# A cross-attention kernel: keys and values by seven quarter products instead of full products, with the work around them spread anew

## The chip, the cores and the metric

The kernel runs on one core of a Trainium2 chip. The metric is the device time of one execution in microseconds (us). Before the change it was 1430.49 us, the median of three runs (1426.22 to 1430.94).

A core has engines that run side by side, each with an instruction queue of its own: TensorE (PE, matrix products; PEld is its weight load), VectorE (DVE), ScalarE (ACT), GpSimd (POOL), and SyncE (SP), whose queue issues the loads and stores here. Data lies in on-chip memory (SBUF, 128 partitions); products land in banks of PSUM and have to be copied or added out of it by VectorE or ScalarE.

## The reference

Two layers run one after the other over x (8 batches x 512 tokens x 512 features) with a context of 8 x 120 rows of 512 features. Each has a gated cross attention and a gated feed-forward part. Cut to what matters (the layer norms, the residuals and the gates belong to the layers' frame):

```python
def _xattn_ref(query_input, key_input, value_input, key_mask, Wq, bq, Wk, bk, Wv, bv, Wo, bo):
    q = _split_heads(query_input @ Wq.T + bq)      # 16 heads of 32
    k = _split_heads(key_input @ Wk.T + bk)
    v = _split_heads(value_input @ Wv.T + bv)
    scores = jnp.einsum('bhqd,bhkd->bhqk', q, k) / jnp.sqrt(jnp.float32(HD))
    scores = jnp.where(mask == 0, jnp.float32(-1e+30), scores)
    attn = jax.nn.softmax(scores, axis=-1)
    ctx = jnp.einsum('bhqk,bhkd->bhqd', attn, v)
    return ctx.transpose(0, 2, 1, 3).reshape(B, -1, D) @ Wo.T + bo

x = x + tanh(g_xattn) * _xattn_ref(layernorm(x), ctx, ctx, ...)
x = x + tanh(g_ffn) * _ffn(layernorm(x))
```

The first layer's attention has no biases and no mask and its feed-forward part routes tokens to experts; the second layer's attention has both, and its feed-forward part mixes each token with the one before it and forms a gated product of 512 x 512 matrices.

## The kernel before

x stays in SBUF for the whole run, as 32 tiles of 128 tokens. The kernel is a sequence of stages: the first attention, the routed experts, the second attention, the channel mix. Each attention (`CrossAttention`) has three parts: a prologue, a loop over token tiles (`run`, lines 635 to 662) and a tail. The change is about the prologue.

**Order of the work.** The whole constructor of `CrossAttention`, with `load`, `project_keys` and `prologue` in it, stands in a block `tc.manual_schedule(engines=every)` (lines 1402 and 1417): on TensorE, VectorE, ScalarE, GpSimd and SyncE the instructions are issued in the order in which the text writes them. In the loop only TensorE (in the second attention SyncE as well) follows the text; a planner orders the other engines by its own costs.

**Loads (`load`, line 263).** The context comes in two halves of four batches (480 rows), then weights and biases. In the first attention the context has to be turned (features onto the partitions) by TensorE (`turn_context`, line 362), and the turned context is written aside to HBM (line 360). The second attention (`self.turned`) loads it from there, twice: into `ctx` for the keys, in two halves, and into `ctxT` for the values. Tiles of the prologue lie in two pools, `at_v` and `at_k`, that begin at the upper end of the memory and reuse the room of the experts' tiles, `permT` (16 KB a partition), `hT` and weights; a load waits until the last reader of what lay there is done.

**Keys (`project_keys`, line 333).** For each half and each of four groups of 128 features: four matmuls of 128 x 128 weights by 480 context rows, summed in one PSUM bank (`kps`, L345), and a copy by ScalarE with the factor 1/sqrt(32) (L354, L358). TensorE runs each of these float32 matmuls as two instructions, so a half has 32.

**Values (`project_values`, line 375).** For each batch four matmuls, 120 context rows by 512 weight columns (`vps`, L379), and an eviction by VectorE, with the bias added in the second attention (L388, L390). After it come the statistics (`bn_stats`, `bn_aggr`, L49 and L50) of four token tiles, and GpSimd's four small instructions for their scales (L58 to L64). In `prologue` three batches come first, three stand between the token tiles' transposes, and the last two come after the scores of token tile 0, between its two parts.

**Queries by seven products.** `SevenProducts` (line 72) multiplies two 512 x 512 matrices, cut into quarters, by seven products of quarters instead of eight, with sums of quarters in front (S1 to S4, `left_steps`; T1 to T4, `right_steps`, each four instructions) and sums behind. Each product, p1 to p7, is four matmuls (eight instructions) into one bank. They run in the order 1, 2, 6, 5, 7, 4, 3. p1 (A11, B11) and p2 (A12, B21) need no sums; p6 needs S2 and T2, the third of the four instructions on each side. p1 and p5 are copied out by ScalarE; p2, p6, p7, p4 and p3 are added by VectorE; after p7 GpSimd adds p5 to two quarters (L192, L193); p4's subtraction has to wait for the first of these and p3's addition for the second. The queries (`queries`, line 465) use it from the start: the weights' sums are made by GpSimd (`sum_query_weights`, L88), the tokens' sums (`start_queries`, L107) by VectorE for the first two batches.

**Tokens.** `normalize` (line 420) has ScalarE write the normalized tile; with biases GpSimd then adds the gated output bias to x (L428). `transpose_x` (line 431) has TensorE turn the tile and ScalarE copy it out (L440). When a batch's four tiles are turned, its query sums follow.

**Scores.** `scores` (line 483) computes the scores of one token tile into the two double banks `s`, VectorE takes the maxima (L532, L543) and subtracts (L545), ScalarE exponentiates (L535, L546). The banks are free for the next scores, or for the transposes of the probabilities (`tps`, L564), only when L535 and L545 have read them. `p_mm` has four further banks, which everything else takes in turn.

## Time and profile before

The profiled execution took 1431.72 us; its span, from the first to the last instruction, is 1429.9 us, and the mean granted TensorE clock 0.995 of full speed.

| what | measured |
|---|---|
| median of three runs | 1430.49 us |
| first attention: first turn of the context to the scores of tile 1 | 9.19 to 91.37 us |
| second attention: first key matmul to the scores of tile 1 | 693.25 to 768.91 us |
| key matmuls of one attention (`kps`, L345, second attention) | 64 in 26.03 us |
| value matmuls of one batch (`vps`, L379) | 8 in 3.43 us |
| TensorE busy from 104 to 200 us, in the first loop | 95.0 of 96.0 us |
| TensorE busy from 790 to 900 us, in the second loop | 110.0 of 110.0 us |

How to read the lines that follow in this document. A page gives the busy time of each engine and its share of the span; the chain that ended last is followed back from the last instruction, at each step to what released it. A line of the instructions in order of time has the start (us from the span's start), the length, the engine, the line of the kernel, the operation, output tile <- input tiles, the shape, and in brackets the idle time of the engine before it with what ended it. Matmuls are pipelined, so the times of single ones overlap; the distance from start to start is what counts.

### The profile page before, as it was taken

The page shows a single profiled execution, that of the slowest core. Times are in us where ns is not written, and L with a number is a line of the kernel's source. Part 1 is how long each engine was busy: PE and PEld are TensorE (multiplying, and loading weights), DVE is VectorE, ACT ScalarE, POOL GpSimd, SP SyncE. Part 2 cuts the span into 40 slices and gives each one's busy share as a digit, 9 for nine tenths or more (in the row PEclk, how much of TensorE's full clock was granted, in tenths as well). Part 3 has the DMA queues.
Part 4 walks back from the last instruction along what each step waited for, and adds up shares of the span by engine and source line. Part 5 has one row for each costly group of instructions (what it writes and reads, how often), then busy time and mean ns, then how long its engine had stood idle before and what let it go on. Part 6 is the DMA issues. An engine that isn't in the chain of part 4 may idle for free.

```text
span 1429.9 us, 32488 instructions
## 1 busy us (share of the span) xinstructions
PE 1383.4 (97%) x13696; PEld 1067.2 (75%) x13696; DVE 1020.5 (71%) x1453; ACT 768.2 (54%) x1870; POOL 644.0 (45%) x576
## 2 busy tenths in 40 slices
PE   7999999999999997999999999999998999999997
PEld 3577777777776787888657777777776788888886
DVE  2666777777777676777566777777777588887786
ACT  1256666666666445444225665666566555445543
POOL 1425545545444000555375575565546333343331
PEclk9999999999999999999999999999999999999999
DMA  9400000000001337432501000000000000000001
GB/s 301 162 9 24 24 23 23 24 23 16 24 31 43 131 125 227 133 106 87 173 0 60 2 2 1 2 2 2 2 30 2 1 30 30 30 30 30 30 16 45
DMA packets 45240, 73.39 MB, mean 51 GB/s; under 512 B 2925, under 2 KB 21869, under 8 KB 44837
## 3 DMA queue, kind: packets, MB, share of 16 engines
q1 hardware_dynamic: 44805, 71.30, 15.0%
q8 instruction: 108, 1.77, 0.5%
q14 instruction: 39, 0.32, 0.1%
q10 hardware_dynamic: 288, 0.00, 0.0%
HBM read 52.55 MB, written 18.74 MB: 50 GB/s over the span
## 4 chain that ended last, share of the span: by engine, by line
PE 72%; DVE 14%; ACT 6%; POOL 4%; issue 3%; DMA 1%; POOLq 0%; SPq 0%; DVEq 0%; ACTq 0%
PE ops L616 15%; PE qps L149 13%; PE tps L564 6%; PE cps L149 5%; PE aps L599 5%; PE s L507 4%; PE kps L345 4%; PE rps L1010 3%; PE vps L379 3%; PE l1ps L925 2%; PE rlps L749 2%; PE ops L1031 2%; PE gps L898 2%; PE xnps L439 2%; DVE rT L990 2%
## 5 line engine op out<-in xcount | busy, mean ns | idle before, releaser
L525 POOL TENSOR_TENSOR pr<-pr,rs 128x960 f32<-128x960 f32 x128 | 229.4, 1795 | 253.2 <-DVE rs L524 231.7
L616 PE MATMUL ops<-wo,aT 128*128 128x512 f32 x512 | 240.6, 596 | 0.7 <-ACT aT L607 0.7
L535 ACT ACTIVATE pr<-s,nmx 128x120 f32<-128x120 f32 x512 | 176.8, 371 | 114.0 <-DVE nmx L532 110.1
L616 PEld LDWEIGHTS ops<-wo,aT 128*128 128x128 f32 x512 | 92.6, 191 | 72.5 <-issue 67.8
L1023 POOL TENSOR_TENSOR r<-r,b 128x1024 f32<-128x1024 f32 x31 | 73.5, 2377 | 145.2 <-ACT r L1022 145.2
L149 PE MATMUL qps<-xnT,wq 128*128 128x256 f32 x512 | 119.6, 381 | 0.0
L564 PEld LDWEIGHTS tps<-ident,pr 128*120 128x120 f32 x864 | 96.7, 138 | 29.6 <-issue 26.2
L543 DVE TENSOR_REDUCE mx<-s 128x8 f32<-128x960 f32 x64 | 74.0, 1156 | 56.6 <-PE s L507 56.6
L535 ACT ACTIVATION_READ_ACCUMULATOR pr<-s,nmx 128x1 f32 x512 | 111.1, 217 | 0.0
L564 PE MATMUL tps<-ident,pr 128*120 128x128 f32 x864 | 104.9, 273 | 2.5 <-ACT pr L535 1.3
L149 PEld LDWEIGHTS qps<-xnT,wq 128*128 128x128 f32 x512 | 95.7, 189 | 15.2 <-issue 1.0
L551 DVE TENSOR_REDUCE sm<-pr 128x8 f32<-128x960 f32 x64 | 73.5, 1148 | 21.9 <-ACT pr L546 21.8
L49 DVE BATCH_NORM_STATS2 bnst<-x 128x6 f32<-128x512 f32 x128 | 86.8, 678 | 1.3
L440 ACT COPY xnT<-xnps 128x512 f32<-128x512 f32 x64 | 38.1, 595 | 82.0 <-PE xnps L439 82.0
L532 DVE TENSOR_REDUCE nmx<-s 128x8 f32<-128x960 f32 x64 | 73.5, 1148 | 8.3 <-PE s L507 8.3
L599 PE MATMUL aps<-prT,v 120*32 120x128 f32 x2048 | 73.3, 278 | 4.1 <-ACT prT L589 2.2
L545 DVE TENSOR_TENSOR pr<-s,mx 128x960 f32<-128x960 f32 x64 | 73.5, 1149 | 0.9
L1276 POOL TENSOR_TENSOR x<-x,cv 128x512 f32<-128x512 f32 x28 | 41.5, 1480 | 70.7 <-DVE cv L1273 70.7
L574 ACT COPY prT<-tps 120x1024 f32<-120x1024 f32 x54 | 55.0, 1019 | 32.7 <-PE tps L564 32.7
L507 PE MATMUL s<-kT,qT 32*128 32x120 f32 x2048 | 71.9, 278 | 0.0
L507 PEld LDWEIGHTS s<-kT,qT 32*128 32x128 f32 x2048 | 66.5, 188 | 6.5 <-issue 6.3
L599 PEld LDWEIGHTS aps<-prT,v 120*32 120x32 f32 x2048 | 53.8, 110 | 18.3 <-issue 8.6
(191 smaller groups left out, 3088.2 us busy)
## 6 DMA issues: line engine op xcount, KB each, us to landing
w<-in_w_dram SPq DMA_DIRECT2D x32, 512.0 KB, 4.8
x<-in_x_dram SPq DMA_DIRECT2D x8, 1024.0 KB, 15.4
aside<-x SPq DMA_DIRECT2D x32, 256.0 KB, 2.0
x<-aside SPq DMA_DIRECT2D x8, 1024.0 KB, 10.5
out_dram<-x SPq DMA_DIRECT2D x14, 512.0 KB, 2.8
wk<-in_wk_dram SPq DMA_DIRECT2D x3, 1024.0 KB, 8.8
wv<-in_wv_dram SPq DMA_DIRECT2D x3, 1024.0 KB, 5.6
wq<-in_wq_dram SPq DMA_DIRECT2D x2, 1024.0 KB, 15.7
```

Of the source, the lines that this page charges most:

```text
L49: cm.nc.vector.bn_stats(st, cm.x[:, t, :])
L149: self.nc.tensor.matmul(ps[:, m, :], self.a[a][:, k, m * P : (m + 1) * P], self.b[b][:, k, :], start=(k == 0), stop=(k == 1),)
L507: nc.tensor.matmul(s[j // 2][:, j % 2, hc * LK : (hc + 1) * LK], self.qT[b][r : r + 32, hc, toks], self.kT[r : r + 32, hc, keys], start=no ...
L525: nc.gpsimd.tensor_tensor(pr[:, js, :, :], pr[:, js, :, :], rs[:, js, :, :].to_broadcast([P, 2, NC, LK]), ALU.mult,)
L532: nc.vector.tensor_reduce(nmx, sv[1], AX.X, ALU.max, negate=True)
L535: nc.scalar.activation(pr[:, 2 + j, hc, :], sv[1][:, j, hc, :], AF.Exp, bias=nmx[:, j, hc, :], accum_out=sm[:, 2 + j, hc : hc + 1],)
L543: nc.vector.tensor_reduce(mx, sv[0], AX.X, ALU.max)
L545: nc.vector.tensor_tensor(pv, sv[0], mx.to_broadcast([P, 2, NC, LK]), ALU.subtract)
L551: nc.vector.tensor_reduce(sm[:, :2, :], pv, AX.X, ALU.add)
L564: nc.tensor.transpose(ps[:, jj, hc * P : (hc + 1) * P], pr[:, 2 * u + jj, hc, :], self.cm.ident,)
L599: nc.tensor.matmul(aps[32 * j : 32 * j + 32, hc, :], self.v[b // 2][:LK, b % 2, h * HD : (h + 1) * HD], prT[:, j, hc, :], start=True, stop ...
L616: nc.tensor.matmul(ops, self.aT[t][:, c, :], self.wo[:, c, :], start=(c == 0), stop=(c == NC - 1),)
```

## The change

- Keys and values are computed with `SevenProducts` too, one object for each half of the context (480 rows): seven products of 256 x 256 weight quarters by 256 x 240 context quarters for the keys (28 matmuls, 56 instructions, of 240 columns, where there were 32 instructions of 480); for the values the context quarter is the stationary side (120 rows, two batches) and the weight quarter the moving one (256 columns). `turned=LK` exchanges the sides.
- New sums: four of the key weights on VectorE, four of each context half on GpSimd (used by keys and values), four of the value weights on GpSimd. New sums behind: GpSimd adds twice after each p7, as for the queries, for two key and two value halves.
- The context is one tile for each half, used by keys and values. The second attention loads it once instead of twice; its second half is loaded behind the biases of queries and keys and the value weights. The write aside in the first attention becomes two.
- The factor 1/sqrt(32) moves from the keys' copy to the tokens' copy (L440) and to the query bias. The value bias of the second attention is added in two parts (one on p1, one after p7, with `bvmore`, the difference of the bias halves); keys and queries use `bias(n)`.
- The statistics no longer come in batches of four tiles: `pieces` puts one or two behind each product. The gated output bias, the normalization of the first two tiles and the query weights' sums move behind the keys or behind the first half of the values.
- All values are computed before the queries. Behind the scores of tile 0, before their softmax, come the transposes and normalizations of three token tiles (`tokens`).
- The query tile is allocated when the batch is turned, and holds T3 until p7; the tile `xns` falls away. The tiles of the attention's second half (`prT`, `aT`) and the channel mix's `r` lie in a pool `late`, opened after the prologue.

```diff
         ps = self.psum()
+        rows, columns, n = self.a[a], self.b[b], P
+        if self.turned:
+            rows, columns, n = columns, rows, self.turned
         for m in range(2):
             for k in range(2):
                 self.nc.tensor.matmul(
                     ps[:, m, :],
-                    self.a[a][:, k, m * P : (m + 1) * P],
-                    self.b[b][:, k, :],
+                    rows[:, k, m * n : (m + 1) * n],
+                    columns[:, k, :],
...
-        for m in range(2):
-            self.nc.scalar.activation(
-                self.q1[:, m, :], ps[:, m, :], AF.Identity, bias=self.bias[0][:, m : m + 1]
-            )
+        else:
+            self.bias[0](self.q1, ps)
     def p2(self):
         ps = self.multiply("A12", "B21")
...
         if self.bias is None:
             nc.vector.tensor_tensor(u3, u2, ps, ALU.add)
         else:
-            for m in range(2):
-                more = self.bias[1][:, m : m + 1]
-                nc.vector.scalar_tensor_tensor(
-                    u3[:, m, :], ps[:, m, :], more, u2[:, m, :], ALU.add, ALU.add
...
                 self.project_keys()
-                if self.biased:
-                    nc.gpsimd.tensor_scalar(self.gbo, self.gbo, self.gate, None, ALU.mult)
-                for t in range(2):
-                    self.normalize(t)
                 if self.masked:
                     self.make_mask()
-                self.sum_query_weights()
-                for b in (1, 2):
-                    self.stats_of_batch(b)
             self.work = pool("at_work", 2)
             self.prologue()
+        self.late = pool("at_late", 2)
...
-        self.ctxT = vp.tile([P, NC, B * LK], FP, name="ctxT")
+        half, own = B * LK // 2, 3 if self.turned else 4
+        self.ctxT = [vp.tile([P, NC, half], FP, name=f"ctxT{h}") for h in range(2)]
+        self.csums = [vp.tile([P, own, 2, half // 2], FP, name=f"cs{h}") for h in range(2)]
+        self.q5 = vp.tile([P, 2, 256], FP, name="cq5")
         wv = self.soft.tile([P, NC * D], FP, name="wv", tag="pr")
         self.wv = wv.rearrange("p (c f) -> p c f", c=NC)
+        wvs = self.soft.tile([P, NC * D], FP, name="wvs", tag="pr")
+        self.wvs = wvs.rearrange("p (n k s) -> p n k s", n=4, k=2)
         if self.biased:
             self.bv = vp.tile([LK, D], FP, name="bv")
-        if self.turned:
-            self.ctx = kp.tile([P, NC, B * LK], FP, name="ctx")
-        else:
+            self.bvmore = vp.tile([LK, D // 2], FP, name="bvmore")
...
         half(0)
         weights(self.wk, wkT)
-        half(1)
         if self.biased:
             bqk_in, bv_in, bo_in = biases
             self.bqk = self.pool.tile([P, 2, NC], FP, name="bqk")
             nc.sync.dma_start(out=self.bqk, in_=bqk_in)
-        weights(self.wv, wvT)
         if self.turned:
-            nc.sync.dma_start(out=self.ctxT, in_=self.aside)
+            weights(self.wv, wvT)
+            half(1)
+        else:
+            half(1)
...
+    def value_bias(self):
+        if not self.biased:
+            return None
+        nc = self.nc
+        def wide(b):
+            return b.unsqueeze(1).to_broadcast([LK, 2, D // 2])
+        def first(q, ps):
+            nc.vector.tensor_tensor(q, ps, wide(self.bv[:, : D // 2]), ALU.add)
+        def more(q, ps, u):
+            nc.vector.tensor_tensor(q, ps, u, ALU.add)
+            nc.vector.tensor_tensor(q, q, wide(self.bvmore), ALU.add)
+        return first, more
...
+    def sum_context(self, h, engine):
+        n = B * LK // 4
+        if self.turned:
+            sums = [quarter(self.ctxT[h], 0, 1, n)]
+            sums += [self.csums[h][:, i] for i in range(3)]
+        else:
+            sums = [self.csums[h][:, i] for i in range(4)]
+        for step in SevenProducts.right_steps(self.ctxT[h], *sums, engine, n=n):
+            step()
+        return SevenProducts.right(self.ctxT[h], *sums, n=n)
+    def sum_weights(self, w, sums, engine):
+        sums = [quarter(w, 0, 1)] + sums
+        for step in SevenProducts.left_steps(w, *sums, engine):
+            step()
+        return SevenProducts.left(w, *sums)
+    def keys(self, h):
+        n = B * LK // 4
+        kT = self.kT[:, :, 2 * n * h : 2 * n * (h + 1)]
+        return SevenProducts(
+            self.nc,
+            lambda: self.p_mm.tile([P, 2, n], FP, name="kps", tag="mm"),
+            self.wk7,
+            self.ctx7[h],
+            {(i, j): quarter(kT, i, j, n) for i in (0, 1) for j in (0, 1)},
+            lambda: self.q5[:, :, :n],
+            bias=self.bias(1),
+        )
+    def values(self, h):
+        return SevenProducts(
+            self.nc,
+            lambda: self.p_mm.tile([LK, 2, 256], FP, name="vps", tag="mm"),
+            self.wv7,
+            self.ctx7[h],
+            {
+                (i, j): self.v[2 * h + j][:LK, :, 256 * i : 256 * i + 256]
+                for i in (0, 1) for j in (0, 1)
+            },
+            lambda: self.q5[:LK],
+            bias=self.value_bias(),
+            turned=LK,
+        )
...
+    def pieces(self, product, n, stats):
+        for _ in range(n):
+            product.next()
+            for _ in range(stats):
+                self.stats(next(self.unmeasured))
+    def project_keys(self):
+        nc = self.nc
+        self.unmeasured = iter(range(NT))
+        self.ctx7 = [None, None]
+        if not self.turned:
+            for b in range(4):
+                self.turn_context(b)
+        self.wk7 = self.sum_weights(self.wk, self.wks, nc.vector)
+        self.ctx7[0] = self.sum_context(0, nc.gpsimd)
+        k = self.keys(0)
+        self.pieces(k, 2, 0)
+        if not self.turned:
+            for b in range(4, B):
+                self.turn_context(b)
+            self.ctx7[1] = self.sum_context(1, nc.gpsimd)
+        self.pieces(k, 1, 0)
+        self.pieces(k, 2, 1)
+        if self.turned:
+            self.ctx7[1] = self.sum_context(1, nc.gpsimd)
+        self.pieces(k, 2, 1)
+        k = self.keys(1)
+        self.pieces(k, 5, 1)
+        self.wv7 = self.sum_weights(self.wv, [self.wvs[:, i] for i in range(3)], nc.gpsimd)
+        self.pieces(k, 2, 1)
+        if not self.turned:
+            for h in range(2):
+                keys = slice(h * B * LK // 2, (h + 1) * B * LK // 2)
+                nc.sync.dma_start(out=self.aside[:, :, keys], in_=self.ctxT[h])
+    def prologue(self):
+        nc = self.nc
+        if self.biased:
+            nc.gpsimd.tensor_scalar(self.gbo, self.gbo, self.gate, None, ALU.mult)
+            nc.vector.tensor_tensor(
+                self.bvmore, self.bv[:, D // 2 :], self.bv[:, : D // 2], ALU.subtract
             )
-        v = self.v[b // 2][:LK, b % 2, :]
-        if self.biased:
-            nc.vector.tensor_tensor(v, ps, self.bv, ALU.add)
-        else:
-            nc.vector.tensor_copy(v, ps)
-        if b + 3 < B:
-            self.stats_of_batch(b + 3)
-    def prologue(self):
-        for b in range(3):
-            self.project_values(b)
-        for t in range(2 * TB):
+        v = self.values(0)
+        self.pieces(v, 5, 1)
+        self.sum_query_weights()
+        self.pieces(v, 2, 1)
+        for t in range(2):
+            self.normalize(t)
+        v = self.values(1)
+        for t in range(TB):
+            self.pieces(v, 1, 1 + (t < 2))
             self.transpose_x(t)
             self.normalize(t + 2)
-            if t < TB - 1:
-                self.project_values(t + 3)
-            elif t < 2 * TB - 1:
-                self.queries(0, t + 1 - TB)
-        rest = self.scores(0)
-        for b in range(B - 2, B):
-            self.project_values(b)
-        rest()
+        self.pieces(v, 3, 1)
+        for f in range(NC):
+            self.queries(0, f)
+            for t in self.unmeasured:
+                self.stats(t)
+                if t % 2:
+                    break
+        self.transpose_x(TB)
+        self.normalize(TB + 2)
+        def tokens():
+            for t in range(TB + 1, 2 * TB):
+                self.transpose_x(t)
+                self.normalize(t + 2)
+        self.scores(0, tokens)()
...
-        nc.scalar.copy(self.xnT[b][:, :, i * P : (i + 1) * P], ps)
+        dst = self.xnT[b][:, :, i * P : (i + 1) * P]
+        nc.scalar.activation(dst, ps, AF.Copy, scale=SM_SCALE)
...
-        own = self.work.tile([P, 2, 256], FP, name="xns", bufs=1)
-        sums = [quarter(xnT, 0, 1), quarter(xnT, 0, 0), own, quarter(xnT, 1, 0)]
+        self.qT[b] = self.work.tile([P, NC, S], FP, name="qT")
+        last = quarter(self.qT[b], 1, 0)
+        sums = [quarter(xnT, 0, 1), quarter(xnT, 0, 0), last, quarter(xnT, 1, 0)]
...
+        if between is not None:
+            between()
```

## The prediction

> **What bounds the kernel now.** I read the page's busy times and chain first, then TensorE's, GpSimd's and VectorE's instructions in order of time through the two prologues, the only places whose work changes, and last the granted clock in stretches where TensorE idles.
>
> ```profile
> PE 1383.4 (97%) x13696; PEld 1067.2 (75%) x13696; DVE 1020.5 (71%) x1453; ACT 768.2 (54%) x1870; POOL 644.0 (45%) x576
> PE 72%; DVE 14%; ACT 6%; POOL 4%; issue 3%; DMA 1%; POOLq 0%; SPq 0%; DVEq 0%; ACTq 0%
> ```
>
> TensorE bounds the whole, so a matmul saved is time saved wherever TensorE does not then wait. Its order in the second prologue (start, length):
>
> ```profile
> 693.25 26.03 PE L345 MATMUL kps<-ctx,wk 128*128 128x480 f32 x64
> 719.12 10.46 PE L379 MATMUL vps<-wv,ctxT 128*120 128x512 f32 x24
> ...
> 741.46 3.62 PE L149 MATMUL qps<-xnT,wq 128*128 128x256 f32 x16
> ...
> 746.64 1.97 PE L149 MATMUL qps<-xnT,wqs 128*128 128x256 f32 x8 [1.12 <-POOL nmr L64]
> ...
> 756.76 0.38 PE L497 MATMUL s<-mbias,ones 1*128 1x480 bf16 x4
> 756.97 1.05 PE L507 MATMUL s<-kT,qT 32*128 32x120 f32 x32
> 757.96 7.13 PE L379 MATMUL vps<-wv,ctxT 128*120 128x512 f32 x16
> ...
> 768.91 0.38 PE L497 MATMUL s<-mbias,ones 1*128 1x480 bf16 x4
> ...
> 774.28 1.06 PE L564 MATMUL tps<-ident,pr 128*120 128x128 f32 x8 [0.45 <-DVE pr L545]
> ```
>
> Two things to see. The one long wait, 1.12 us, is on GpSimd, whose queue is already late. And the last two value products (7.13 us) lie between the first scores and the second: they fill the time in which the first softmax empties its banks. The first prologue is alike: scores at 79.33, values 80.42 to 87.55, second scores at 91.37, transposes at 96.74. GpSimd and VectorE there:
>
> ```profile
> 720.81 2.50 POOL L428 TENSOR_TENSOR x<-x,gbo 128x512 f32<-128x512 f32 x2 [12.71 <-ACT xn L424]
> 723.25 0.20 POOL L330 MEMSET ones<- 128x128 bf16 x1
> 723.41 1.28 POOL L88 TENSOR_TENSOR wqs<-wq 128x512 f32<-128x512 f32 x1
> ...
> 753.60 1.18 POOL L192 TENSOR_TENSOR qT<-qT,xnT 128x512 f32<-128x512 f32 x1
> ```
> ```profile
> 742.28 1.70 DVE L107 TENSOR_TENSOR xns<-xnT 128x512 f32<-128x512 f32 x1
> ...
> 757.49 0.69 DVE L107 TENSOR_TENSOR xns<-xnT 128x512 f32<-128x512 f32 x1 [0.30 <-ACT xnT L440]
> ```
>
> GpSimd works in the order of the text: it stood 12.71 us at L428 with ready weight sums behind it. A sum costs it 1.27 us, 1.35 with its gap; four statistics' scales take 2.03 (728.85 to 730.89). A VectorE sum of two SBUF operands takes 0.69, but 1.70 beside GpSimd's L428 (742.16 to 743.43): one waits out the other.
>
> **Matmuls.** 64 of 480 columns took 26.01 us, 0.406 each; at 240 columns I take half, so a product (8 matmuls) takes 1.63 and half the keys 7 x 1.63 = 11.4 for 13.0. If the weight loads (0.19) bound them, 1.73 as for the queries, 1.4 us more per attention. A value product is a query product by shape, 3.46 / 2 = 1.73: half the values 12.1 for 13.7. Saved: 6.4 us per attention, 12.8 in all, were all else hidden.
>
> **First prologue.** Weights land at 12.25 (issue 1.25 + 11.0), the second half of the context at 17.2 (1.71 + 15.5). The first two products run 12.65 to 15.9; TensorE waits for the context to 17.2. The turns' copies and p2's add stand on VectorE behind four weight sums, which alternate with GpSimd's context sums to 18.8, so the turns end at 20.0 and p6 starts at 20.2. Statistic 0 needs x, landed at 22.4 (3.11 + 19.3), before p7's add at 25.1: hidden. Keys end at 39.8 (before 41.85). Value sums end their third at 43.7, TensorE waits 0.4; values end at 66.3 with four token turns (0.44 each). The query's T2 follows p2's add: 1.4 of wait. Seven query products, one token turn: scores at 80.3, 1.0 later than before, with all values done. GpSimd's last value adds are on time here (65.8). The spread statistics (0.80) and an eviction (0.69) make 1.49 of VectorE's time per product of 1.63 or 1.73: hidden; without that cover, what exceeds the product.
>
> Then the cover is gone. Three token turns follow; ScalarE copies and normalizes (0.48 + 0.75 each) in front of the exponentials, and VectorE does two query sums before the maximum. Scores 80.3 to 81.4, last copy 84.9, sums 86.3, maximum 87.3, eight exponentials (2.8) 90.1: only then are the banks free. TensorE has finished turns, two query products and a turn by 87.6 and idles 2.5. Second scores at 90.1 (before 91.37): **-1.2 us** of the 6.4.
>
> **Second prologue.** Loads: by the tiles' sizes the first context half lies 32.0 to 24.3 KB below the top of memory, clear of the routing's permT (top 18.6 KB), so its load goes at 667 as now, and the key weights' behind it. On SP the second half moves behind the key and query biases (690.8, as now) and the value weights (691.2); it reaches permT, so it goes at 693.3, as ctxT does, and lands before 703. Were the first held too, 5.3 us more. One load of ctxT falls away.
>
> TensorE and GpSimd step by step from 693.3:
> - Two key products to 696.6. p6 needs the third sum of VectorE and of GpSimd, three times about 1.8 in turns: 698.7, wait 2.1 (if the weight sums are done earlier, 0.5).
> - p7 at 703.6, its two adds of L189's kind 0.9, GpSimd's adds to 706.9, then the second context sums: third at 710.7. TensorE would be there at 710.1: wait 0.6. Keys end 718.9 (before 719.28).
> - GpSimd: fourth sum 712.0, scales 714.0, scales 716.7, adds 719.0, value-weight sums, third at 723.05 (wait 0.7), fourth 724.4. Values of half 0 end at 731.8.
> - GpSimd goes on: ones and gbo (1.58) 726.2, scales 728.2, p7's adds 729.7 to 732.0, scales 734.0, query-weight sums 739.4, two L428 (1.33 each) 742.1, scales 744.1, three L428 748.1, scales 750.1, L428 751.4. Only now come the two adds of half 1's p7: 752.5 and 753.7. TensorE had that p7 at 742.2 and VectorE at 743.6: **7.8 us late**.
> - VectorE in text order stands at p4's subtraction until 752.5. Behind it: a statistic, p3's add, a statistic, the query's p2 add, T2: 753.2, 754.0, 754.6, 755.4, 756.1, 756.8.
> - TensorE ends half 1 at 745.6, two query products at 749.1, and waits for T2 to 756.9, where it now starts p6 at 746.64. Five products and a turn: scores at 766.0, **+9.2**.
> - Fill as above, with GpSimd's L428s between the sums: second scores 11.4 after the first (before 12.15): **-0.7**.
>
> **The clock after the wait.** Stretches of 5 us (length, busy PE, PEld, DVE, ACT, POOL; then PEclk, DMA, GB/s):
>
> ```profile
> 1080.00:1085.00 5.00, 2.47 (x19) 1.69 (x18) 4.71 (x7) 4.79 (x20) 1.22 (x2) 0.97 0.00 0
> 1085.00:1090.00 5.00, 5.00 (x69) 3.94 (x70) 2.64 (x4) 1.61 (x3) 4.92 (x4) 0.50 0.01 3
> ```
>
> Half idle, then half clock: the score matmuls at 1087.69 took 1.91 for 1.05. A wait of 7.8 us should do the same; between nothing and 5 us of half clock, thus 0 to 2.5 lost, I take **+2.0**, near the full row since this wait is the longer; the short fills 0 to 1.5, **+0.5**. The Trainium skill's "TensorE: Matmul & The Clock Gate" (What's actually happening) wants a whole idle window of some 3.4 us before half rate; the 2.47 busy of 5 above disagree in that less idleness sufficed. By its rule the short fills would cost nothing, and the estimate would be 0.5 us lower.
>
> **Elsewhere.** The token copy with a scale: L358 0.57 as against L371 0.56, 10 ns on ScalarE, which was busy 63.7 of 96 us from 104 to 200; without that cover 64 x 0.01 = 0.6. T3 in the query tile waits for scores two batches back, whose matmuls run earlier in the same step. L59, L64 and L428 stay as many. The two aside writes replace one of equal bytes on SP, long before wc's load at 87.6. Other reorderings by the planner: I keep +-2.
>
> A rule speaks against the change: the Trainium skill's "GPSIMD Engine Reference" (3.1, Elementwise) gives about 2.6 cycles an element on GpSimd, twice VectorE's time. By it a sum of 512 would be an estimate of 1.11 us; over the 29 such instructions on this queue before the late adds the lateness would be some 4.6 us less, and so would the sum. The row of 1.27 decides.
>
> **Sum.** -1.2 + 9.2 - 0.7 + 2.0 + 0.5 = +9.8 us. The profiled execution took 1431.72 us (span 1429.9), 1.2 above the median of 1430.49. On the median: 1440.
>
> **Rivals.**
> 1. *GpSimd keeps up.* Its idle time or shorter instructions give back the 7.8 us. The 1.12 us wait speaks against: less is queued there now. Then query p6 goes at 750.5, scores at 759.6 (+2.8), fill as in the first prologue (9.8 for 12.15, -2.3), second prologue +0.5, total -0.7: 1430.
> 2. *Faster: the queues run by readiness, not by the text.* Where the value adds pass L428 and the maximum passes the token sums, the lateness goes, and so do the two fill waits of some 2.5: 1430 - 5 = 1425. It decides once the adds run before 744. The 12.71 us at L428 speak against.
> 3. *Worse.* More is held: first context load with permT (+5.3), or a key product at 1.73 (2.8 in both). 1446.
>
> **How the numbers follow.** Forecast 0.62, own range 1435 to 1445 (sums and clock bounds: 2.1 to 0.5 at the first wait, 0 to 4 of clock, +-2 planner); rival 1 0.20, rival 2 0.08, rival 3 0.10. From 1428 to 1448 at most 2 in 10 lie outside. A measurement tells about 0.3% (4.3 us) from no change: faster, below 1426.2, 0.08; slower, above 1434.8, the forecast's and rival 3's with some loss to the middle, 0.71; same 0.21.
>
> **What would show it.** Second prologue: the value adds of half 1 on GpSimd start 6 to 9 us after VectorE's p7 add; a TensorE wait of 6 to 9 us in the queries, released by the sum at L107's successor; half clock behind it; second scores about 8 to 11 us late against the start of the keys. First prologue: second scores within 2 us of 91.4, an idle of some 2.5 before them. Key matmuls at 0.20. The forecast is wrong if GpSimd has idle time between the query-weight sums and the late adds, or if its order is not the text's.

## The result, and the profile after

The changed kernel takes 1442.92 us (median of six runs, 1442.38 to 1445.77), the kernel before 1430.72 (six runs beside it, 1426.22 to 1431.96): ratio 1.0095, 95% interval 1.0079 to 1.0112, 12.2 us slower. The forecast was 1440, range 1428 to 1448. The profiled execution took 1443.25 us, its span is 1441.5: 11.6 more than before.

Busy times and the chain, from the page after:

```profile
PE 1376.2 (95%) x13888; PEld 1106.3 (77%) x13888; DVE 1054.1 (73%) x1492; ACT 765.9 (53%) x1870; POOL 694.7 (48%) x616
PE 67%; DVE 16%; ACT 7%; POOL 6%; issue 3%; DMA 1%; SPq 0%; POOLq 0%; DVEq 0%; ACTq 0%
```

TensorE is busy 7.2 us less over a span 11.6 us longer: it stands still 18.8 us more. On the chain it falls from 72 to 67%, GpSimd and VectorE rise by two points each. The second prologue shows where (TensorE in order of time: start, length, line, tiles, idle time before):

```profile
692.21 3.51 PE L156 MATMUL kps<-ctxT,wk 128*128 128x240 f32 x16
697.44 1.86 PE L156 MATMUL kps<-cs,wks 128*128 128x240 f32 x8 [1.73 <-DVE wks L88]
...
717.99 3.62 PE L156 MATMUL vps<-wv,ctxT 128*120 128x256 f32 x16
...
745.19 3.62 PE L156 MATMUL qps<-xnT,wq 128*128 128x256 f32 x16
757.50 3.75 PE L156 MATMUL qps<-xnT,wqs 128*128 128x256 f32 x8 [8.69 <-DVE xnT L107]
761.05 2.49 PE L156 MATMUL qps<-xnT,wq 128*128 128x256 f32 x8
...
769.09 0.38 PE L600 MATMUL s<-mbias,ones 1*128 1x480 bf16 x4
...
780.58 0.59 PE L600 MATMUL s<-mbias,ones 1*128 1x480 bf16 x4 [3.70 <-ACT pr L640]
...
782.79 3.63 PE L156 MATMUL qps<-xnT,wqs 128*128 128x256 f32 x8
...
793.13 0.38 PE L600 MATMUL s<-mbias,ones 1*128 1x480 bf16 x4
```

The saving is there: keys and values are done 52.98 us after the first key matmul (692.21 to 745.19), where before only six of eight value batches were done at 48.2 (741.46 less 693.25) and the last two cost 7.13 us later. Then 8.69 us are lost at one place, in front of p6 of the queries, and 3.70 in front of the second scores. A query product takes 3.55 us (757.50 to 761.05) and 3.47 (782.79 to 786.26) after these waits, 1.72 undisturbed. GpSimd, then VectorE, at the long wait:

```profile
739.52 2.50 POOL L528 TENSOR_TENSOR x<-x,gbo 128x512 f32<-128x512 f32 x2
...
744.98 3.71 POOL L528 TENSOR_TENSOR x<-x,gbo 128x512 f32<-128x512 f32 x3
...
750.68 1.26 POOL L528 TENSOR_TENSOR x<-x,gbo 128x512 f32<-128x512 f32 x1
751.90 1.26 POOL L192 TENSOR_TENSOR v<-v,cq 120x512 f32<-120x512 f32 x1
753.12 1.27 POOL L193 TENSOR_TENSOR v<-v,cq 120x512 f32<-120x512 f32 x1
```
```profile
743.94 0.69 DVE L364 TENSOR_TENSOR v<-v,bvmore 120x512 f32<-120x512 f32 x1
...
753.20 0.69 DVE L198 TENSOR_TENSOR v<-v,vps 120x512 f32<-120x512 f32 x1 [7.74 <-POOL v L192]
...
756.67 1.41 DVE L107 TENSOR_TENSOR xnT<-xnT 128x512 f32<-128x512 f32 x2
```

VectorE is done with p7 (L364) at 744.6; GpSimd, in the order of the text, does six adds to x and the scales between them first, and comes to the value adds at 751.90. VectorE stands 7.74 us at p4's subtraction, with T2 of the queries behind it, and TensorE waits for T2. Nobody needs the adds to x soon. The chain of waits says the same: from 739.6 to 753.2 it runs on GpSimd alone, then on VectorE to T2 at 757.4, then comes p6.

The first prologue (TensorE):

```profile
38.61 3.62 PE L156 MATMUL vps<-wv,ctxT 128*120 128x256 f32 x16
...
70.68 1.97 PE L156 MATMUL qps<-xnT,wqs 128*128 128x256 f32 x8 [1.54 <-DVE xnT L107]
...
79.92 1.17 PE L610 MATMUL s<-kT,qT 32*128 32x120 f32 x32
...
90.14 2.08 PE L610 MATMUL s<-kT,qT 32*128 32x120 f32 x32 [2.53 <-ACT pr L640]
92.15 3.78 PE L156 MATMUL qps<-xnT,wqs 128*128 128x256 f32 x8
...
102.69 1.17 PE L610 MATMUL s<-kT,qT 32*128 32x120 f32 x32
```

The second scores start 1.2 us earlier than before, at 90.14; they run at half clock (2.08 for 1.17). The third ones start at 102.69, 0.94 later than the 101.75 of before. The granted clock in stretches (length, busy PE, PEld, DVE, ACT, POOL; then PEclk, DMA share, GB/s):

```profile
88.00:92.00 4.00, 1.86 (x32) 1.80 (x32) 3.77 (x6) 4.00 (x16) 1.53 (x1) 0.73 0.00 0
92.00:96.00 4.00, 4.00 (x14) 3.13 (x10) 3.97 (x5) 0.17 (x1) 2.01 (x2) 0.50 0.00 0
...
750.00:755.00 5.00, 0.00 (x0) 0.00 (x0) 1.77 (x4) 0.00 (x0) 4.22 (x6) 0.70 0.00 0
755.00:760.00 5.00, 2.50 (x6) 2.08 (x7) 3.81 (x9) 0.00 (x0) 0.92 (x2) 0.50 0.61 211
...
780.00:785.00 5.00, 4.42 (x41) 3.81 (x41) 4.74 (x7) 2.60 (x7) 3.84 (x3) 0.50 0.00 0
```

Each of the three waits is followed by half clock while TensorE has work. But the half clock is not what makes the stretch from the second scores to the third longer. VectorE in the first attention, after and then before:

```profile
90.24 2.83 DVE L107 TENSOR_TENSOR xnT<-xnT 128x512 f32<-128x512 f32 x2
93.00 1.14 DVE L656 TENSOR_REDUCE sm<-pr 128x8 f32<-128x960 f32 x1
...
94.30 1.11 DVE L648 TENSOR_REDUCE mx<-s 128x8 f32<-128x960 f32 x1
```
```profile
91.70 1.69 DVE L107 TENSOR_TENSOR xnT<-xnT 128x512 f32<-128x512 f32 x1
93.32 1.14 DVE L543 TENSOR_REDUCE mx<-s 128x8 f32<-128x960 f32 x1
```

After the change two query sums and the sum of tile 0's probabilities (L656) stand between the start of the second scores and the maxima of tile 1, where before only one query sum stood there. VectorE comes to these maxima 4.16 us after the second scores began, before 1.95 (in the second attention 4.15 and 1.95), and the transposes of the probabilities wait for what follows the maxima. The experiments below settle that this, and not the clock, is the 2.17 of the following balance, stage by stage:

| stretch | before | after | difference |
|---|---|---|---|
| start to second scores, first attention | 91.37 | 90.14 | -1.23 |
| second to third scores, first attention | 10.38 | 12.55 | +2.17 |
| to the first key matmul of the second attention | 591.50 | 589.52 | -1.98 |
| from there to p6 of the queries | 53.39 | 65.29 | +11.90 |
| p6 to first scores | 10.12 | 11.59 | +1.47 |
| first to second scores | 12.15 | 11.49 | -0.66 |
| second to third scores | 10.38 | 12.55 | +2.17 |
| from there to the end | 650.6 | 648.4 | -2.2 |

### The profile page after: what moved, and what is told of

Same layout as the page of the kernel before. It is cut to its first block, busy times and chain, and to the rows that moved or that the text cites. A ratio compares the mean times of both kernels' runs of the same rounds, so it can differ in the third digit from the quotient of the medians.

```text
span 1441.5 us, 33010 instructions
## 1 busy us (share of the span) xinstructions
PE 1376.2 (95%) x13888; PEld 1106.3 (77%) x13888; DVE 1054.1 (73%) x1492; ACT 765.9 (53%) x1870; POOL 694.7 (48%) x616
## 4 chain that ended last, share of the span: by engine, by line
PE 67%; DVE 16%; ACT 7%; POOL 6%; issue 3%; DMA 1%; SPq 0%; POOLq 0%; DVEq 0%; ACTq 0%
PE ops L721 14%; PE qps L156 13%; PE tps L669 6%; PE cps L156 5%; PE aps L704 4%; PE s L610 4%; PE rps L1115 3%; PE rlps L854 2%; PE l1ps L1030 2%; PE ops L1136 2%; PE vps L156 2%; DVE rT L1095 2%; PE gps L1003 2%; ACT pr L640 2%; DVE cv L1378 2%
## 5 line engine op out<-in xcount | busy, mean ns | idle before, releaser
L656 DVE TENSOR_REDUCE sm<-pr 128x8 f32<-128x960 f32 x64 | 73.6, 1150 | 22.0 <-ACT pr L651 21.8
L156 PE MATMUL qps<-xnT,wqs 128*128 128x256 f32 x256 | 68.8, 414 | 10.2 <-DVE xnT L107 10.2
L541 ACT ACTIVATE xnT<-xnps 128x512 f32<-128x512 f32 x64 | 38.8, 607 | 55.7 <-PE xnps L539 55.7
```

The costliest lines, as they stand in the source:

```text
L156: self.nc.tensor.matmul(ps[:, m, :], rows[:, k, m * n : (m + 1) * n], columns[:, k, :], start=(k == 0), stop=(k == 1),)
L656: nc.vector.tensor_reduce(sm[:, :2, :], pv, AX.X, ALU.add)
```

## The experiments

The prediction's account (theory A): the loss lies in the second attention, in the value adds that stand on GpSimd behind the adds to x; half clock after the waits adds to it; the two waits before the second scores take the rest. Against it stand accounts in which TensorE would lose as much with the adds on time: the wait only moves, or the loss comes from the products and their sums themselves. In those the first two kernels below stay near 1440 or 1443. The first four kernels share 28 runs of the kernel before (median 1430.12), the last four 19 (1429.74). The changed kernel had 1430.72 beside it, so differences from its 1442.92 can be off by up to 1 us for that alone.

**The adds to x later.** The six adds L528 of the first tiles are held back and issued behind the last piece of the values.

```diff
         if self.biased:
-            nc.gpsimd.tensor_tensor(cm.x[:, t, :], cm.x[:, t, :], self.gbo, ALU.add)
+            def add():
+                nc.gpsimd.tensor_tensor(cm.x[:, t, :], cm.x[:, t, :], self.gbo, ALU.add)
+            self.held.append(add) if self.hold else add()
...
         self.pieces(v, 3, 1)
+        self.hold = False
+        for add in self.held:
+            add()
         for f in range(NC):
```

> The changed kernel, but in the second attention the six additions of the output bias to x (1.25 us each on GpSimd) that stand ahead of the second value half's two late additions are written behind them. The work is the same, only its place in GpSimd's queue differs. If the queue's order is the cause (theory A), the late additions start about 7.5 us earlier, TensorE's wait in the first query products falls from 8.69 us to about 1.5 (what it is in the first attention, 1.54), the half clock behind it goes, and the total is about 9.5 us less: 1433. If the amount of GpSimd's work is the cause (rival B), the moved additions hold up the next thing on that queue, the query's own two additions or the softmax's multiplications, and less than 3 us are won: 1440 or more. If VectorE's own list is what is late (rival C), nothing moves: 1443.

Measured: 1434.85 us (ten runs), ratio 1.0033 (1.0020 to 1.0045), 8.1 us faster than the changed kernel. GpSimd, then TensorE:

```profile
745.81 1.27 POOL L192 TENSOR_TENSOR v<-v,cq 120x512 f32<-120x512 f32 x1
747.03 1.27 POOL L193 TENSOR_TENSOR v<-v,cq 120x512 f32<-120x512 f32 x1
748.26 8.29 POOL L533 TENSOR_TENSOR x<-x,gbo 128x512 f32<-128x512 f32 x6
```
```profile
752.68 3.56 PE L156 MATMUL qps<-xnT,wqs 128*128 128x256 f32 x8 [2.51 <-DVE xnT L107]
...
775.10 0.38 PE L606 MATMUL s<-mbias,ones 1*128 1x480 bf16 x4 [3.70 <-ACT pr L646]
```

The wait falls from 8.69 to 2.51; the same work, only in another order, is worth 8.1 us by the medians. The trace, which is of the slowest of the ten runs (1439.15), has the third scores 94.11 us after the first key matmul, for 100.92. An account in which the loss does not hang on the adds is out. The 1.0 us more than the expected wait of 1.5: the adds are still 1.2 late, behind the query-weight sums and two groups of scales, and T2 on VectorE now runs beside the held adds (1.17 us on the chain of waits, 0.61 after). The expectation that the half clock goes was wrong: it sets in behind the shorter wait too (p6's line has 3.56), and from p6 to the first scores it takes 10.93 us, where the next two kernels, at full clock, need 9.24.

**The value adds on VectorE.** Half 1's two adds after p7 in the second attention go to VectorE; GpSimd keeps its order.

```diff
             lambda: self.q5[:LK],
             bias=self.value_bias(),
+            engine=self.nc.vector if self.turned and h == 1 else None,
```

> The changed kernel, but the two additions behind p7 of the second value half are VectorE's in the second attention, not GpSimd's. Theory A: they no longer stand behind 7.7 us of other work; on VectorE each takes 0.69 us, or up to 2 beside a GpSimd sum, so they are done some 4 to 6 us earlier and the wait of 8.69 us falls to 2 to 4; total 1434 to 1437. Rival C (VectorE's own list is late): the wait stays or grows, since VectorE now has more to do: 1443 or more.

Measured: 1436.82 us (nine runs), 1.0045 (1.0031 to 1.0060), 6.1 faster than the changed kernel.

```profile
753.28 1.97 PE L156 MATMUL qps<-xnT,wqs 128*128 128x256 f32 x8 [2.19 <-POOL rstd L59]
```

Once more the lateness goes, although GpSimd has the rest of its work in the old order. So GpSimd's order and load matter here only through these two adds. The bracket names GpSimd's scales, but p6 reads nothing of them: T2 on VectorE ended at 753.13, 0.12 us before p6's first weight load, the same distance as in the changed kernel. VectorE works without a pause from the value adds to T2, so its own list is what is late now.

The first attention is the same code in this kernel and in the changed one, and here no half clock falls behind its second scores until 99.9 us. TensorE, at full clock:

```profile
90.73 1.17 PE L611 MATMUL s<-kT,qT 32*128 32x120 f32 x32 [2.53 <-ACT pr L641]
...
98.26 1.06 PE L670 MATMUL tps<-ident,pr 128*120 128x128 f32 x8 [2.71 <-DVE pr L651]
```

It is ready earlier and then stands 2.71 us for VectorE; the first transposes of probabilities come 7.53 us after the second scores, with 6.8 us of half clock (changed kernel) 7.78, before the change 5.37. In the second attention the distance is 7.53 or 7.54 in the changed kernel (6.8 us of half clock) and in the first three experiments (3.4 us). From the second scores to the third it is 12.55 in all of these eight cases but this kernel's first attention, which has 13.41: there 3.4 us of half clock fell on the transposes themselves.

**Keeping TensorE busy in the wait.** 64 extra transposes into a spare bank, whose output nobody reads, stand behind the query's p2 in the second attention; all else is as in the changed kernel.

```diff
             self.queries(0, f)
+            if f == 0 and self.turned:
+                spare = self.p_s.tile([P, 2, 512], FP, name="warm", tag="s")
+                for _ in range(64):
+                    nc.tensor.transpose(spare[:, 0, :P], self.cm.ident, self.cm.ident)
```

> The changed kernel, with 64 transposes of the identity matrix (0.109 us each, 7.0 us) put into TensorE's wait of 8.69 us in the second attention; their output is not used. This measures what the half clock behind the wait costs. If it costs what the rows say, the query's p6 starts at the same time, but it and p5 take 1.73 us each and not 3.55 and 2.33, the first scores come 2.4 us earlier, and the total is 1440.5. If the slow products are covered by the work of VectorE and GpSimd on the statistics and sums, the total stays at 1443.

```profile
747.13 7.15 PE L499 MATMUL warm<-ident 128*128 128x128 f32 x64
756.05 1.97 PE L156 MATMUL qps<-xnT,wqs 128*128 128x256 f32 x8 [1.77 <-DVE xnT L107]
```

p6 starts at the same place (65.36 us after the first key matmul at 690.69, for 65.29), but at full clock: the first scores come 74.60 after that matmul, for 76.88. The clock behind the long wait costs 2.3 us (taken in the prediction: 2.0). The median falls only by 1.6, to 1441.35 (1.0074, 1.0060 to 1.0089); the runs cannot tell 1.6 from 2.3.

**Another order in the fill.** The two query sums of batch 1 go behind the first softmax's maxima and subtraction, the normalizations of tiles 8 and 9 behind its exponentials.

```diff
-        for step in steps[:2]:
+        self.first_sums = steps[:2] if b == 1 else []
+        for step in steps[:2] if b != 1 else []:
             step()
...
                 self.transpose_x(t)
-                self.normalize(t + 2)
-        self.scores(0, tokens)()
+                if t == TB + 1:
+                    self.normalize(t + 2)
+        rest = self.scores(0, tokens)
+        for t in (2 * TB, 2 * TB + 1):
+            self.normalize(t)
+        for step in self.first_sums:
+            step()
+        rest()
```

> The changed kernel, with another order on VectorE and ScalarE after the first scores, in both attentions: the two query sums of the next batch stand behind the softmax's maxima and subtraction, and the normalizations of tiles 8 and 9 behind the exponentials. TensorE's order is unchanged. If the waits before the second scores (2.53 and 3.70 us) come from that order (theory A), they fall below 1 us each, and with them the half clock behind them (6.8 us each, about 2 us of work each): total 1435 to 1438. If the first softmax is simply longer than the work left to cover it (rival D), the wait moves to the next turn of a token tile or to the transposes of the probabilities, and at most 2 us are won: 1441.

Measured: 1432.08 us (twelve runs), 1.0015 (1.0004 to 1.0026), 10.8 faster than the changed kernel: the expectation was too small.

```profile
752.61 3.75 PE L156 MATMUL qps<-xnT,wqs 128*128 128x256 f32 x8 [8.70 <-DVE xnT L107]
...
772.54 0.66 PE L545 MATMUL xnps<-ident,xn 128*128 128x128 f32 x4 [1.55 <-ACT xn L530]
773.13 0.38 PE L607 MATMUL s<-mbias,ones 1*128 1x480 bf16 x4
```

The long wait stays (8.70), the waits before the second scores (2.53 and 3.70) are gone, and a wait of 1.55 or 1.56 for a normalized tile stands in their place. Waits alone give 3.1 us of gain. From the start of the attention to its third scores the trace gains 3.5 and 5.2, 8.7 together. The other 5.6 lie between the second scores and the third (9.63 and 9.86 us, for 12.55 in both): with the query sums done earlier, VectorE comes to the maxima of tile 1 1.20 and 1.42 us after the second scores began, for 4.16 and 4.15. The half clock behind these waits is gone too, but by the traces above it had cost nothing at the third scores. The remaining 2 us of the median lie outside both prologues and are not traced to a place.

**One attention alone.** The changed class for the first layer and the class of before (`OldCrossAttention`) for the second, and the other way round. Only the line that changes is shown.

```diff
-    attention = CrossAttention(
+    attention = OldCrossAttention(
```

> The changed attention in the first layer alone; the second layer's attention is that of before. By the profile of the changed kernel the first prologue gives back all that its products save: the scores of the third token tile come at 102.7 us for 101.75 before. Theory A expects the total 1 to 1.5 us over that of before: 1431.5. If the 2.3 us by which the second attention's keys then start earlier than that belong to the change, and not to the phase in which the clock falls in the experts' part, it is 1 us under: 1429.

> The changed attention in the second layer alone; the first layer's attention is that of before. Theory A expects nearly the whole loss here: the scores of the third tile 14.9 us later against the start of the keys, less some 2 us that the part after it had less half clock in that one execution: 1443, against 1430 before. If the two attentions share the loss, it is 1436.

Measured: first layer alone 1429.27 us (twelve runs), 0.9993 (0.9981 to 1.0005), no change; second alone 1445.63 (six runs), 1.0100 (1.0081 to 1.0118), with the waits of 8.70 and 3.69 in its trace. So the whole loss lies in the second attention. Theory A's 1431.5 for the first layer alone was wrong: the interval ends 0.7 us above the time before. The trace of this run has the third scores at 103.37, 1.6 late, and yet the second attention begins at 693.2, as before; what gave the 1.6 us back was not traced step by step. A likely source: the trace of before has 3.4 us of half clock from 545.4, with TensorE busy throughout, worth 1.7, and this one has none between its third scores and the second attention. The matmuls saved in the first attention show as no gain that these runs can tell.

**Both orders, and what they leave.** `x_late_fill` has the adds to x late and the new fill. `best` adds, in the second attention, the second context half's sums ahead of the first half's p6; and in both attentions the value weights' sums after the third piece of the second keys, tile 4's turn between the query's p2 and p6, and tile 8 normalized before the exponentials.

```diff
+        if self.turned:
+            self.ctx7[1] = self.sum_context(1, nc.gpsimd)
         self.pieces(k, 1, 0)
         self.pieces(k, 2, 1)
-        if self.turned:
-            self.ctx7[1] = self.sum_context(1, nc.gpsimd)
         self.pieces(k, 2, 1)
         k = self.keys(1)
-        self.pieces(k, 5, 1)
+        self.pieces(k, 3, 1)
         self.wv7 = self.sum_weights(self.wv, [self.wvs[:, i] for i in range(3)], nc.gpsimd)
-        self.pieces(k, 2, 1)
+        self.pieces(k, 4, 1)
...
             self.queries(0, f)
+            if f == 0:
+                self.transpose_x(TB)
+                self.normalize(TB + 2)
...
-        self.transpose_x(TB)
-        self.normalize(TB + 2)
```

> Both changes of order together: the six bias additions behind the value additions, and the query sums and two normalizations behind the softmax's first part. If the two waits are separate costs, as theory A has it, the gains of 8.1 and 10.8 us add up: 1424, faster than before. If the one wait only stands in for the other (taking one away lets VectorE or GpSimd be late at the other place), the sum is no better than the better of the two: 1432.

> The last one, and four small waits of the changed kernel taken away by order alone: in the second attention the second context half's sums stand before the first keys' additions on GpSimd and the value weights' sums before the second keys' additions (waits 0.78 and 1.02 us); a token tile's turn stands between the query's p2 and p6 (0.44 us in each attention); tile 8 is normalized before the exponentials, tile 9 after (waits of 1.55 us in each attention). If each is worth its wait, 3 to 5 us less than the last one: 1420. If the waits only move to the next thing in line, 1424.

Measured: `x_late_fill` 1425.87 us (eight runs), 0.9968 (0.9954 to 0.9981); `best` 1423.54 (six runs), 0.9956 (0.9940 to 0.9973). Both are faster than the kernel before, by 0.3 and 0.4%. The two orders' gains nearly add: 8.1 and 10.8 alone, 17.05 of 18.9 together. In `best` the waits for the sums of context and value weights (0.78, 1.02) and for tile 8 are gone, but the query's wait grew from 2.51 to 3.20, although a turn now lies inside it:

```profile
744.12 3.17 PE L156 MATMUL qps<-xnT,wqs 128*128 128x256 f32 x8 [3.20 <-DVE xnT L107]
```

TensorE gets there earlier, and the chain of waits again runs over GpSimd (query-weight sums, scales, L192) and VectorE to T2. Each wait taken away early comes back in part at the next engine that is late. The intervals of the two kernels overlap, so the 2.3 us between their medians are not shown to be a gain. In the traces the third scores come 1.9 and 1.6 us earlier in the two prologues, yet the spans are alike (1423.4 and 1423.5), and the trace of `best` has 6.8 us of half clock near 1080 that the other lacks. The median lies nearer to the expectation of moved waits (1424) than to that of separate ones (1420).

## Why the prediction was right

**The forecast's case came.** TensorE bounds the whole, GpSimd keeps the order of the text, p4's subtraction could start at 753.20 (predicted 752.5; counted from the first key matmul, 61.0 for 59.2), and TensorE waited 8.69 us for T2 (predicted 7.8). The first two experiments show the cause of the long wait by taking it away in two ways.

**Matmuls.** A key product takes 1.62 us from start to start (702.38 to 704.00; taken 1.63), a value product 1.73 (as taken). Rival 3's slow key product, and its held first load, did not come.

**First prologue.** Step by step: keys end 38.61 (39.8), wait at the values 0.73 (0.4), values end 65.52 (66.3), wait at T2 1.54 (1.4), scores 79.92 (80.3), idle before the second scores 2.53 (2.5), second scores 90.14 (90.1). The term of -1.2 was exact and yet not the end of it: 2.17 were lost until the third scores.

**Second prologue.** The waits at p6, at the second context sums and at the value weights were 1.73, 0.77 and 1.02 (2.1, 0.6, 0.7). Queries' p6 came 65.29 after the first key matmul (predicted 63.6, since 756.9 less 693.3): +11.9 instead of +10.3 against before, mostly the 0.9 by which the wait was longer and the 0.7 by which the values ended later. The fill's -0.7 was measured as -0.66. GpSimd's sums took 1.26 to 1.30 us undisturbed, as the row of 1.27 had it. The 1.11 us worked out from the Trainium skill's "GPSIMD Engine Reference" (3.1, Elementwise) is too short by these rows. The 4.6 us that the prediction hung on it were too many even by that figure: GpSimd stood idle for 1.95 us until 729.67, so only the 12 such sums between there and the late adds could have shortened the lateness, by an estimated 12 x 0.16 = 1.9 us.

**The clock was sized right, and a term was missing.** Predicted were +2.0 after the wait and +0.5 for the short fills. Measured are 2.3 after the wait (the run with extra transposes) and nothing to be seen at the third scores after the fills: 12.55 us from the second scores with 6.8 us of half clock as with 3.4, since TensorE would have stood for VectorE instead. What the sum lacks is the stretch behind the second scores. It ends each prologue there and takes what follows as unchanged, without a reason, though it had itself noted that the cover for VectorE's work is gone. The query's later two sums and the sum of the probabilities now stand ahead of the softmax of tile 1, and the stretch took 2.17 longer in each attention, 4.3 in all. The new fill, which moves query sums forward, takes this away.

Where the half clock sets in is another matter. The Trainium skill's "TensorE: Matmul & The Clock Gate" (What's actually happening) asks for a whole idle window of about 3.4 us before half rate, in windows that run free of the program. The long wait agrees; the fills with 2.53 and 3.70 us of idleness, the first of them clearly shorter than such a window, do not, and the measurement decides.

**Elsewhere, +-2.** Outside the prologues the trace after is 4.2 us shorter (1.98 and 2.2). Before had 10 us at half clock there (545 to 550 and 1085 to 1095), after had none. Half of 10 us, 5, would more than account for it. But over the ten traces the two stretches run from 588.1 to 591.5 and from 647.2 to 650.7, and which execution meets half clock there changes from run to run (below), so this is a likely source and not a shown one. The sum: -1.2 + 11.1 (the 13.4 to the first scores without 2.3 of clock) + 2.3 - 0.7 + 4.3 - 4.2 = +11.6, against +9.8. That the total came so near is in part luck: the 4.3 that the prediction did not see and the 4.2 elsewhere cancel.

**The rivals.** Rival 1 (GpSimd keeps up, 1430) fell with the 7.74 us. One argument that the prediction held against it was a misreading: the wait of 1.12 before p6 in the kernel before, put on GpSimd's L64 by its bracket, ended with T2 on VectorE (745.78 to 746.50; the weight load follows 0.12 later, as after), so it says nothing of GpSimd's queue. Rival 2 named the right two places: with the adds ahead of L528 and the maximum ahead of the token sums it gave 1425, and the kernel that does both by another text order takes 1425.87; its sum had only the waits, so the nearness is in part luck. The queues do not do it by themselves.

## What to carry to other kernels

A saved matmul is worth its time only where the sums before and behind it are on time. On an engine that follows the text, look for work that nobody waits for (here the adds to x) in front of work that somebody does; putting it behind cost nothing and was worth 8 us. Follow a change past the place where it acts: here the sums moved out of cover also held up the next softmax, for 2.2 us in each attention. And ask of half clock whether TensorE is the late engine while it lasts: behind the long wait it was, and it cost 2.3 us; behind the fills of the changed kernel VectorE was later still, and it cost nothing that shows.

## What the runs showed of the hardware that was not expected

The half clock comes in pieces of about 3.4 us or whole multiples: in the trace after about 6.8 us from 89.8, 10.2 from 752, 6.8 from 779.3. It set in 3.2 us after TensorE had stopped at 748.8, but only 2.2 and 2.4 after it had stopped at 87.6 and 776.9; in the 3.4 us ahead of these two onsets TensorE was busy for 1.2 and 1.0 us.

Where it falls differs between executions of the same code. The first attention is the same in the changed kernel and in the first three experiments; behind its first fill the traces show 6.8 us of half clock from 89.8, 3.4 in the kernels with late adds and with extra transposes, and with the adds on VectorE 3.4 only from 99.9. Where it falls matters more than how long it is: the third scores come 12.55 us after the second in the first three and 13.41 in the last. Over executions up to 1420 us (twice the missing share of the granted clock, in stretches of 5 us) it was 10 us before, 24 after, 17 with late adds, 10 with the adds on VectorE, 14 with extra transposes, 10 with the new fill, 3 with both orders, 10 in `best`. Half of such a time is the most that it can cost; a difference of 2 us between two single traces may thus be this alone.

VectorE's sums of two SBUF operands slow down beside GpSimd's (L107 1.63 us at 740.95 beside L528, 0.69 the next), as the prediction read from before. It works both ways: GpSimd's L59, 1.04 us elsewhere, took 1.45 at 742.75.
